# Idle products of the identity on TensorE between the two recurrences of a recommender kernel

## The chip, the cores and the metric

The kernel runs on one core of one Trainium2 chip. The metric is device time in microseconds (us) of the whole launch, the median of three runs. Below, PE is TensorE, DVE is VectorE, ACT is ScalarE, POOL is GpSimd and SP is SyncE. PEld is TensorE's weight load, and the clock is the share of TensorE's full speed that was granted.

## The reference

1024 users have a history of 100 items of 128 numbers each, in float32. A GRU runs over the history, an attention net scores its states against a query item, and a second recurrence (AUGRU) runs over the states with an attention weight a step. A small net ends it.

```python
_, gru_seq = jax.lax.scan(gru_step, h0, jnp.swapaxes(item_historical_embedding, 0, 1))
keys = jnp.swapaxes(gru_seq, 0, 1)
...
attn = jax.nn.softmax(score, axis=1)[..., 0]
pooled = jnp.einsum('bt,btd->bd', attn, keys)
att_seq = pooled.T[:T]

def augru_step(h, inp):
    x_t, a_t = inp
    ti = jnp.concatenate([h, x_t], axis=-1)
    r = jax.nn.sigmoid(ti @ aug_Wr.T + aug_br)
    u = jax.nn.sigmoid(ti @ aug_Wu.T + aug_bu)
    h_hat = jnp.tanh(jnp.concatenate([h * r, x_t], axis=-1) @ aug_Wh.T + aug_bh)
    u = a_t[:, None] * u
    h_new = (1.0 - u) * h + u * h_hat
    return (h_new, h_new)
_, aug_seq = jax.lax.scan(augru_step, h0, (jnp.swapaxes(keys, 0, 1), att_seq))
```

The weights a_t of the second recurrence are the columns of pooled, so step 0 of it needs pooled in full, which is known only when the first recurrence and the attention over all of its states are done. A user's result is the state at the end of his own history.

## The kernel before

The work has two phases, each a recurrence over 100 steps on two halves of 512 users. In the first, `gru_phase`, the GRU, the attention net and an online softmax run side by side; the states go to DRAM as keys_d. Its end (lines 888 to 956) empties the pipeline: the last attention scores, the last sums into pooled on POOL (half 0) and DVE (half 1), eight products of user features (`features`, line 630, PE's last work of the phase, in the two PSUM banks `banks["f"]`), and the store of pooled to DRAM as pooled_d.

The second, `augru_phase`, treats the users sorted by length, so that later steps are narrower. Between the phases stands a branch on a count of users, taken by every engine. Then, in the program's order:

- `load_key` (1047) for steps 0 to 3: PE transposes gathered states (L1055), ACT copies them to SBUF (L1056). `first_step` (986): gates of step 0 from the input alone, four products of 128x512 on PE (L996), sigmoid and tanh on ACT (L998).
- ACT issues three of the stores of pooled_d, SP the other five (L956). `gather_weights` (1002): POOL gathers rows of pooled_d in sorted order, four indirect DMAs a half (L144), as `att_r`. Then POOL gathers the states of later steps (L174), sixteen for half 1 with nothing between them, and from then on some each half step, each behind a copy (L173) that waits for DVE's `rest`, which sets their pace.
- `open_gates` (1068): the input's part of the three gates of step 1 (L1073). `close_gate` (1075) later adds the state's part (L1077).
- `first_state` (1019) for half 0: `weight_row` (1008) makes the row of weights of step 0 for 512 users by four row products with the identity (L1011), each of which waits for one gather; DVE multiplies it with the two gates (L1022, L1023), which gives the state after step 0. `first_weights` (1025): the same for step 1, copied by ACT (L1028).
- `half_step` (1088) for step 1 and half 0: products pr and pu on that state, sigmoids on ACT (L1097, L1098), DVE's r (L1103). `store_weights` (1030): PE transposes att_r (L1033), DVE copies it (L1035), SP stores it and loads the weights of later steps from there. Then `first_state` for half 1, with row products into the bank `spare`. In half 1's half step, `open_state` (1080) makes ph and its tanh (L1085), and pr and pu of half 1 follow, which read the state of L1023.

Each engine works in its program's order: on PE a product that waits holds all products behind it. In float32 a product is two records of the profile, a transpose one. The order is written by hand; waits are put in for it.

Of the kernel before, what the change touches and what calls it, by code (L numbers as in the profile page):

```python
# [19 lines left out]
P = 128  # L20
# [58 lines left out]
def kernel(ctx: ExitStack, tc: tile.TileContext, a: dict, out: bass.AP):  # L79
# [26 lines left out]
    nc = tc.nc  # L106
# [21 lines left out]
    ident = const.tile([P, P], F32, name="ident")  # L128
# [53 lines left out]
    def all_of(steps):  # L182
        for _ in steps:
            pass

    def gru_phase(pools):
        wih = const.tile([P, 3, P], F32, name="wih")
# [468 lines left out]
        def blocked(t):  # L656
            return t.rearrange("p (k r) -> p k r", r=R)
# [4 lines left out]
        banks = {}  # L662
# [164 lines left out]
        for s in range(T):  # L827
            last = s == T - 1
            n, due = divmod(s - again, 4)
            n, i = divmod(n, NH)  # L830
# [55 lines left out]
            if more_history and due == 2:  # L886
                halves[i].history(n)
        all_of(rest)

        b = [ps.tile([P, HB], F32, tag="g", name="last") for _ in range(6)]  # L890
# [23 lines left out]
        n = ENDS[-3] - ENDS[-4] + 1  # L914
# [30 lines left out]
        halves[0].pool(T, nc.gpsimd)  # L945
        halves[1].pool(T, nc.vector)
        all_of(more_early)


        for half in reversed(halves):  # L950
            t = blocked(s_bs[NH * (soft["j"] % 2) + half.i])
# [6 lines left out]
    def augru_phase(pools, widths, alive):  # L958
# [46 lines left out]
                gather(r[:, g, :], pooled_d, g, i)  # L1005
            return r

        def weight_row(t, i, p):

            for g in range(GH):  # L1010
                nc.tensor.matmul(  # L1011
                    p[:, ts(g, P)],
                    lhsT=sorted_rows[i][:, g, t : t + 1].to_broadcast([P, P]),
                    rhs=ident,
                    start=True,
                    stop=True,
                )

        def first_state(i, p):
            weight_row(0, i, p)  # L1020
            u, h = gates[i]
            nc.vector.tensor_mul(p, p, u)  # L1022
            nc.vector.tensor_mul(h3[i], p, h)  # L1023

        def first_weights(i, p):
            weight_row(1, i, p)
            at = att[1, i] = wp.tile([P, HB], F32, name="at", bufs=6)
            nc.scalar.copy(at, p)  # L1028
# [59 lines left out]
        def half_step(t, i):  # L1088
# [17 lines left out]
            if t == 1 and i == 0:  # L1106
                store_weights(0, pa.tile([P, HB], F32, tag="a", name="pw"))
                first_state(1, spare)
            elif t == 1:
                first_weights(1, spare)  # L1110
# [118 lines left out]
        for to, t in later["att", 0][: G - 1]:  # L1229
            nc.scalar.dma_start(out=to, in_=t)  # L1230
        sorted_rows = [gather_weights(i) for i in range(NH)]
        all_of(load_rows(1, 1, widths[FIRST[1]], kp))
        for i in range(NH):
            load_key(2, i, (FREE_BANK, None)[i])
        open_gates(1, 1, EARLY_BANKS)
        open_gates(1, 0, LATE_BANKS)
        for i in range(NH):
            load_key(3, i)
        spare = bank("spare", EARLY_BANKS[-1])
        first_state(0, pa.tile([P, HB], F32, tag="a", name="first"))  # L1240
        first_weights(0, spare)
        ahead, due = gathers(2), spread(2)
# [30 lines left out]
    with ExitStack() as pools, tc.manual_schedule():  # L1273
        gru_phase(pools)
# [79 lines left out]
```

## Time and profile before

| | us |
|---|---|
| median of three runs | 2048.63 |
| the three runs | 2044.19, 2048.63, 2048.96 |
| the profiled execution | 2046.78 |
| its span, first to last instruction | 2045.0 |
| PE busy | 1994.6 (98%) |
| DVE busy | 1682.1 (82%) |
| POOL busy | 1260.7 (62%) |
| ACT busy | 944.1 (46%) |
| mean granted clock of PE | 0.993 |
| last record of the first phase on PE ends | 1404.14 |
| first record of the steady second recurrence | 1460.53 |

The span runs from the first to the last instruction of the profiled execution, and all places are us from its start. A row of a group names line, engine, operation, what is written and read, shape and number of instructions. A time in brackets is idle time of the engine before the instruction, with what ended it.

### The profile page before, as it was taken

The numbers are of one execution on the slowest core, as the hardware profiler recorded it, in microseconds if no ns is written. First come the engines' busy times: TensorE is split into PE (matmuls) and PEld (weight loads), VectorE is DVE, ScalarE is ACT, GpSimd is POOL, SyncE is SP. The second block draws the span as 40 slices with busy tenths as digits, with TensorE's granted clock in tenths as the row PEclk, the third lists the DMA queues.
The fourth block names the chain that finished last, engine by engine and source line by source line (L and its number), as shares of the span: only waits on it lengthen the run. The fifth ranks groups of instructions, "written<-read, shape, count | busy, mean of one in ns | idle before, by whom it ended". The sixth has DMA issues, their size and how long they took to land.

```text
span 2045.0 us, 41241 instructions
## 1 busy us (share of the span) xinstructions
PE 1994.6 (98%) x15452; PEld 1176.7 (58%) x15452; DVE 1682.1 (82%) x3066; ACT 944.1 (46%) x1708; POOL 1260.7 (62%) x1291
## 2 busy tenths in 40 slices
PE   8999999999999999999999999997699999999997
PEld 3655555555555555555555555544344556679997
DVE  6888989888879887878888888996477777878886
ACT  4444444544544454544454444443244444445554
POOL 0233939579796959595969687997543344443431
PEclk9999999999999999999999999999899999999999
DMA  4553333332234334333433232333332333333322
GB/s 118 101 115 97 98 105 113 98 108 86 89 104 114 118 105 119 113 113 97 141 111 97 91 101 69 96 105 108 122 102 91 91 106 103 95 94 86 95 70 36
DMA packets 241645, 205.66 MB, mean 101 GB/s; under 512 B 59271, under 2 KB 204395, under 8 KB 241435
## 3 DMA queue, kind: packets, MB, share of 16 engines
q1 hardware_dynamic: 227498, 170.43, 29.4%
q0 software_dynamic: 12352, 32.31, 5.6%
q8 instruction: 123, 2.02, 0.4%
q14 instruction: 88, 0.71, 0.1%
q10 hardware_dynamic: 1584, 0.20, 0.1%
HBM read 146.82 MB, written 54.40 MB: 98 GB/s over the span
## 4 chain that ended last, share of the span: by engine, by line
PE 92%; DVE 3%; DMA 2%; issue 1%; ACT 1%; another core or an unknown queue 1%; POOL 0%; SPq 0%; DVEq 0%; ACTq 0%; POOLq 0%
PE ps L509 48%; PE pm L673 16%; PE ph L1077 5%; PE pr L1077 5%; PE pu L1077 4%; PE pu L1073 4%; PE ph L1073 4%; PE pr L1073 4%; DMA rows<-keys_d,idx_k 1%; DVE ps L539 0%; DVE u L529 0%; DVE ps L546 0%; DVE d L545 0%; DVE d L544 0%
## 5 line engine op out<-in xcount | busy, mean ns | idle before, releaser
L509 PE MATMUL ps<-x,wih 128*32 128x512 f32 x4800 | 657.2, 594 | 4.4 <-DMA x<-in_hist_x 4.4
L509 PE MATMUL ps<-hn,whh 128*32 128x512 f32 x4752 | 650.1, 592 | 0.6 <-ACT hn L555 0.6
L509 PEld LDWEIGHTS ps<-x,wih 128*32 128x32 f32 x4800 | 281.7, 110 | 241.7 <-issue 220.4
L509 PEld LDWEIGHTS ps<-hn,whh 128*32 128x32 f32 x4752 | 279.6, 110 | 234.2 <-issue 212.0
L494 POOL TENSOR_TENSOR xm<-x,m 128x512 f32<-128x512 f32 x200 | 234.9, 1174 | 146.0 <-DMA m<-mask_d 145.7
L521 ACT ACTIVATE r<-ps,brz 128x512 f32<-128x512 f32 x200 | 137.7, 688 | 394.9 <-PE ps L509 394.7
L495 POOL TENSOR_TENSOR hist<-hist,xm 128x512 f32<-128x512 f32 x200 | 258.7, 1294 | 15.7
L174 POOL DMA_INDIRECT rows<-keys_d,idx_k x220 | 213.2, 969 | 86.2 <-POOL rows L173 48.5
L610 POOL TENSOR_TENSOR pooled<-pooled,kw 128x512 f32<-128x512 f32 x191 | 245.9, 1287 | 15.0
L609 POOL TENSOR_TENSOR kw<-kt,e 128x512 f32<-128x512 f32 x191 | 206.0, 1078 | 70.6 <-DVE e L782 70.6
L673 PE MATMUL pm<-hn,wk 128*32 128x512 f32 x1200 | 237.7, 592 | 5.0 <-ACT hn L555 2.5
L673 PE MATMUL pm<-kq,wkq 128*32 128x512 f32 x1200 | 237.5, 592 | 0.0
L540 ACT ACTIVATE ps<-ps,bih 128x512 f32<-128x512 f32 x200 | 132.4, 662 | 223.9 <-DVE ps L539 223.9
L1085 ACT ACTIVATE c<-ph,bh 128x96 f32<-128x96 f32 (+41 forms) x198 | 96.5, 488 | 295.9 <-PE ph L1077 240.5
L529 DVE SCALAR_TENSOR_TENSOR u<-ps,bhh,r 128x512 f32<-128x512 f32 x198 | 147.5, 745 | 73.1 <-PE ps L509 69.0
L673 PE MATMUL pm<-mv,w 128*32 128x512 f32 (+1 forms) x808 | 197.6, 592 | 0.5 <-ACT mv L712 0.4
L173 POOL COPY rows<-rest 128x1 f32<-128x1 f32 x188 | 35.3, 188 | 217.5 <-DVE rest L1114 213.5
L544 DVE TENSOR_TENSOR d<-hn,ps 128x512 f32<-128x512 f32 x198 | 136.1, 687 | 35.6 <-ACT ps L540 35.2
L1101 DVE TENSOR_TENSOR pu<-pu,c 128x96 f32<-128x96 f32 (+41 forms) x197 | 88.3, 448 | 87.9 <-ACT c L1085 79.8
L545 DVE TENSOR_TENSOR d<-ps,d 128x512 f32<-128x512 f32 x200 | 138.4, 692 | 25.6 <-ACT ps L541 10.9
L555 ACT COPY hn<-ps 128x512 f32<-128x512 f32 x200 | 116.6, 583 | 92.3 <-DVE kq L548 92.3
L539 DVE TENSOR_TENSOR ps<-ps,u 128x512 f32<-128x512 f32 x200 | 140.0, 700 | 21.5 <-PE ps L509 0.5
(181 smaller groups left out, 3235.3 us busy)
## 6 DMA issues: line engine op xcount, KB each, us to landing
x<-in_hist_x SPq DMA_DIRECT2D x212, 256.0 KB
keys_d<-kt SPq DMA_DIRECT2D x48, 1024.0 KB
m<-mask_d SPq DMA_DIRECT2D x200, 128.0 KB
rows<-keys_d,idx_k POOLq DMA_INDIRECT x220
s_b<-mv SPq DMA_DIRECT2D x200, 8.0 KB
keys_d<-kt SPq DMA_DIRECT2D x32, 64.0 KB
at<-att_d SPq DMA_DIRECT2D x34, 48.0 KB
mask_i<-in_mask SPq DMA_DIRECT2D x8, 200.0 KB
```

The costliest lines, as they stand in the source:

```text
L174: nc.gpsimd.indirect_dma_start(out=r[:, at, :], out_offset=None, in_=keys_d[q], in_offset=bass.IndirectOffsetOnAxis(ap=idx_k[:, k, i : i + ...
L494: nc.gpsimd.tensor_mul(d, x, m)
L495: nc.gpsimd.tensor_add(acc, acc, d)
L509: nc.tensor.matmul(p[ts(q, R), :], lhsT=w[:, g, ts(q, R)], rhs=v, start=(j == 0), stop=(j == len(parts) - 1),)
L529: nc.vector.scalar_tensor_tensor(out=u, in0=ph, scalar=bhh[:, 2:3], in1=r, op0=ALU.add, op1=ALU.mult,)
L539: nc.vector.tensor_add(pi, pi, u)
L545: nc.vector.tensor_mul(d, pz, d)
L609: eng.tensor_mul(d, k, w)
L610: eng.tensor_add(acc, acc, d)
L673: nc.tensor.matmul(p[i][s, :], lhsT=w[:, s], rhs=v, start=start, stop=stop)
L1073: nc.tensor.matmul(p, lhsT=m[:, 1, :], rhs=k, start=True, stop=False)
L1077: nc.tensor.matmul(p, lhsT=m[:, 0, :], rhs=v, start=False, stop=True)
```

## The change

A helper issues products of the identity with itself into a PSUM tile. Nine of them follow PE's last product of the first phase, in the bank of an earlier one that has been copied out. Four precede each of the four row products of half 0 at step 0, in the quarter of the tile that the row product then overwrites. For half 1, and for the rows of step 1, none are added. Nothing reads what they write.

```diff
+    def busy(p, n):
+
+        for _ in range(n):
+            nc.tensor.matmul(p[:, :P], lhsT=ident, rhs=ident, start=True, stop=True)
...
         halves[1].pool(T, nc.vector)
         all_of(more_early)
 
+        busy(banks["f"][0], 9)
...
-        def weight_row(t, i, p):
+        def weight_row(t, i, p, idle=0):
 
             for g in range(GH):
+                busy(p[:, ts(g, P)], idle)
                 nc.tensor.matmul(
                     p[:, ts(g, P)],
                     lhsT=sorted_rows[i][:, g, t : t + 1].to_broadcast([P, P]),
...
         def first_state(i, p):
-            weight_row(0, i, p)
+            weight_row(0, i, p, 0 if i else 4)
```

## The prediction

> **What bounds the kernel now.** I read the page first, then the busy time by stage, then the chain of waits and each engine's order of time between 1404 and 1464 us. The page's 40 slices show TensorE (PE) full everywhere but at slices 28 and 29:
>
> ```profile
> PE   8999999999999999999999999997699999999997
> PEclk9999999999999999999999999999899999999999
> ```
>
> The second line, PE's granted clock, dips in the same place. By stage:
>
> ```profile
> 10.00:1378.00 1368.00, 1364.77 (x12708) 740.72 (x12699) 1175.97 (x1795) 646.68 (x1041) 964.28 (x819) 1.00 0.36 104
> 1404.00:1460.00 56.00, 32.43 (x103) 17.61 (x101) 18.32 (x37) 12.86 (x22) 40.39 (x43) 0.79 0.45 126
> 1460.00:2037.00 577.00, 569.87 (x2498) 403.04 (x2498) 464.93 (x1186) 271.12 (x622) 230.19 (x387) 1.00 0.34 91
> ```
>
> The first two columns are stage and length, the next PE's busy time, the seventh PEclk. Both recurrences are PE's (99.8% and 98.8% of their stages), at full clock. The 56 us between are not: 32 us of PE work. A microsecond won there reaches the end whole, since all later work is one PE chain. The clock in steps of 2 us:
>
> ```profile
> 1406.00:1408.00 2.00, 0.00 (x0) 0.00 (x0) 1.60 (x7) 1.51 (x5) 1.92 (x3) 0.97 1.12 354
> 1408.00:1410.00 2.00, 1.99 (x3) 0.96 (x4) 1.97 (x4) 1.25 (x1) 1.92 (x2) 0.50 0.97 294
> 1426.00:1428.00 2.00, 0.97 (x4) 0.59 (x4) 0.00 (x0) 0.00 (x0) 1.45 (x2) 1.00 0.19 51
> 1428.00:1430.00 2.00, 1.22 (x5) 1.22 (x6) 0.32 (x1) 0.00 (x0) 1.39 (x2) 0.59 0.19 47
> ```
>
> Each idle stretch (1405.0 to 1408.0; the gaps of 1424 to 1428) is followed by a half clock: 1407.87 to 1411.29, 1428.35 to 1435.18, and again 1442.01 to 1455.66. PE in order of time (start, length, idle time before it in brackets):
>
> ```profile
> 1425.30 0.46 PE L1011 MATMUL first<-ident,att_r 128*128 128x128 f32 x2 [1.28 <-DMA att_r<-pooled_d,idx]
> 1427.00 0.98 PE L1011 MATMUL first<-ident,att_r 128*128 128x128 f32 x4 [1.25 <-DMA att_r<-pooled_d,idx]
> 1428.78 0.79 PE L1011 MATMUL first<-ident,att_r 128*128 128x128 f32 x2 [0.80 <-DMA att_r<-pooled_d,idx]
> 1429.37 1.91 PE L1011 MATMUL spare<-ident,att_r 128*128 128x128 f32 x8
> ...
> 1435.39 1.06 PE L1011 MATMUL spare<-ident,att_r 128*128 128x128 f32 x8
> 1436.28 1.02 PE L1077 MATMUL ph<-r,wh 128*128 128x510 f32 x2
> 1450.17 2.07 PE L1077 MATMUL pr<-h,wr 128*128 128x510 f32 x2 [12.87 <-DVE spare L1022]
> ```
>
> A row product is two records. The reader should see that the three gaps the change fills are 3.3 us, and that a 12.87 us gap, four times as large, comes later. The chain of waits has it too:
>
> ```profile
> 1437.34 11.32 another core or an unknown queue
> 1448.69 0.71 DVE spare L1022
> ...
> 1454.28 4.19 another core or an unknown queue
> ```
>
> L1022 waits only for PE, for the four row products of half 1, whose records end by 1436.45. The trace's semaphore events tell more. PE's semaphore steps at 1434.94 (pu, on time), then 1436.63, 1437.37, 1440.91, 1445.14, 1448.67, 1453.57 and 1458.47. Matched in order, and by what DVE and ACT do next, these are pw, row products 0 to 3, ph, and pr of half 1. Their records end at 1435.55, 1435.78, 1436.00, 1436.22, 1436.45, 1437.30 and 1452.24, so PE's signals come 1 to 16 us late, one per 3.5 to 4.9 us. At 1459.27 all is caught up. POOL issues a gather every 1.26 us from 1422.48 to 1454.24, 26 on end; the delay starts some 12 us into that run and ends some 3 us behind it. Shorter runs late in the kernel (1822 to 1834, 1935 to 1946) also end with PE signals held, by up to 0.85 us. The trace names no cause.
>
> [...] these f32 records step by 111 and 213 ns, and I use those. [...]
>
> **The change part by part.** The instruction order of both programs shows 25 added products on the path taken and nothing else; the wait for ACT moves from the first row product to the first idle one. Form and price are those of a row product: 8 records in 0.89 us from 1435.39, so 0.22 us each at full clock; 8 in 1.71 us from 1429.37, so 0.43 us at half.
>
> Nine behind the first phase: 1403.98 + 9 x 0.22 = 1405.96. PE's branch work behind them (1401.87 to 1403.05 now) then waits for ACT's copy at 1402.83 + 0.33 and ends near 1404.4, under the idle products. The transposes of L1055 move from 1403.98 to 1405.96; the first four end at 1406.5, the rest at 1407.0. Their reader, ACT's L1056, starts at 1406.88 anyway, held by its own branch, and its second copy at 1407.4. Cost nothing; without ACT's branch as cover, 2.0 us. PE is then idle 1 us instead of 3, so the clock should hold: the four L996 products cost 3.4 us instead of 5.3. But ACT's k copies wait behind its DMA issues until 1417.94, and those wait for pooled. Worth nothing.
>
> Sixteen before half 0's row products: their tile is free at 1424.64. Four cost 0.88, row product 0 starts at 1425.5 (now 1425.30), row product 1 at 1427.0 (its gather), row product 2 at 1428.1, row product 3 at 1429.2 instead of 1428.78, but at full clock: it ends at 1429.6 as now (1429.58). Cost nothing at full clock, 16 x 0.43 - 3.3 of gaps = 3.6 us at half.
>
> Then, with the clock held to 1435: DVE delivers h at 1431.11 as now; pr's signal comes at 1432.1 instead of 1433.24, r at 1433.6 instead of 1434.65, pw at 1433.4, half 1's row products at 1434.0 (the last gather lands at 1433.49) instead of 1436.45. That is the step that matters: 1434.0 is before the delay sets in (1434.94 was on time). DVE's L1022 and L1023 end at 1435.7, and half 1's pr starts at 1435.8 instead of 1450.17.
>
> What is late next? The signals behind it, if the run of gathers, which the change leaves where it is, holds PE's signals whatever PE does. pr of half 1 would take the place of 1437.37, pu 1440.91, first_weights 1445.14, pw 1448.67, ph 1453.57, and pr of step 2 1458.47. Before, that last one came at 1463.8. Gain 5.3 us. The other bound: no delay at all. Then pu of step 2 (L1073, 1460.53) opens at 1439.3, a gain of 21.2. A bound below nothing is rival 4. I take 5.3, because the later runs of gathers show held signals with PE warm and busy.
>
> The sum is made against the profiled execution (2046.78, span 2045.0); the median is 1.85 above it. Differences go to the median: 2048.63 - 5.3 = 2043.3.
>
> **The rivals.**
> 1. Forecast, half a step won: 2043.3, its own range 2038 to 2047. For: the delay follows the run of gathers. Against: the later ones are shorter.
> 2. The delay goes, because it needs a cold or idle PE: 2048.63 - 21.2 = 2027.4. For: it begins at the clock's return at 1435.18 and lasts over an idle, cold PE; elsewhere PE is busy and the delays are under 1 us. Against: other returns of the clock (1411.29) show none.
> 3. The change does not do what it says: the clock falls anyway, or PE's time won is eaten by the same delay. Then half 1's row signals fall into it as now: 2047 to 2049, say 2048.
> 4. Slower: [...] PE is at half clock when the idle products start. Four cost 1.7 us before each row product, row product 3 ends 3.6 us later, at 1433.2, and pr and pu of half 0, on time now, fall into the delay as well. Two more signals wait some 4.2 us there, of which about 3 are left when it ends: 2048.63 + 3.6 + 3 = 2055. It decides if row product 3 ends after some 1431. [...] Against: the trace had the clock full until 1428.35.
>
> **How the numbers follow.** Chances: rival 1 0.36, rival 2 0.22, rival 3 0.22, rival 4 0.20. About 0.3% (6 us) is what a measurement can tell from no change. Half of 1 wins more than that: faster 0.18 + 0.22 = 0.40; same 0.18 + 0.22 = 0.40; slower 0.20. The range goes from rival 2, 2026, to most of rival 4, 2054; some 0.05 lies below, 0.12 above. Faster cases hold most of the chance.
>
> **What would show it.** Right: no half clock at 1407.87 and 1428.35; row product 3 ending near 1429.6; DVE's second L1022 near 1434.3 instead of 1448.69; the wait before ACT's L1097 of half 1 still of unknown origin (case 1) or gone (case 2). Wrong: L1055's ACT copies later than 1406.9, row product 3 later than 1431, or L1022 still near 1448.

## The result, and the profile after

| | before | after |
|---|---|---|
| median, us | 2048.2 (22 runs) | 2051.68 (22 runs) |
| lowest to highest | 2044.19 to 2050.77 | 2047.86 to 2053.26 |
| ratio, 95% interval | | 1.0017 [1.0011, 1.0023] |
| profiled execution | 2046.78 | 2053.26 |
| its span | 2045.0 | 2051.5 |
| last record of the first phase on PE starts | 1403.81 | 1405.89 |
| steady second recurrence opens (pu from the input, step 2) | 1460.53 | 1467.33 |

The change costs 3.5 us: slower by less than my 0.3% bound, and outside my likeliest case. In the kernel after, the lines named in the prediction are 7 higher (L1022 is L1029, L1028 is L1035, L1055 is L1062, L1077 is L1084, L1097 is L1104, L1103 is L1110); the idle products are L189.

The two profiled executions differ by 6.5 us in span. Of these, 2.08 lie ahead of the change: some 1.2 at a half clock of 3.4 us, 27 us into the kernel (26.8 to 30.2), where the trace before has none, and the rest in two small steps later in the first phase. Another 4.7 lie between the last record of the first phase and the steady second recurrence (56.7 and 61.4 us). The rest of the span is 0.3 shorter. So the 4.7 us are to be explained.

The 40 slices of the kernel after, PE's busy share and its clock, show the dip in the same place as before, with PE a tenth busier in one slice and the clock a tenth lower:

```profile
PE   8999999999999999999999999998699999999997
PEclk9999999999999999999999999999799999999999
```

The stages of 2 us (behind the stage, the second figure is PE's busy time and the seventh its clock) show that the idle products did their work. There is no half clock where the kernel before had 0.50 and 0.59, and PE is busy throughout 1428 to 1430:

```profile
1408.00:1410.00 2.00, 1.10 (x11) 0.86 (x9) 1.52 (x7) 1.48 (x4) 1.92 (x3) 1.00 1.12 353
1426.00:1428.00 2.00, 1.34 (x12) 1.20 (x11) 0.00 (x0) 0.57 (x1) 1.69 (x2) 1.00 0.23 66
1428.00:1430.00 2.00, 2.00 (x20) 2.00 (x19) 0.00 (x0) 0.00 (x0) 1.39 (x3) 1.00 0.12 33
```

PE in order of time, with the idle time before an instruction in brackets (the nine idle products are 18 records):

```profile
1406.06 2.17 PE L189 MATMUL last<-ident 128*128 128x128 f32 x18
1408.07 1.04 PE L1062 MATMUL pk<-ident,rows 128*128 128x128 f32 x8
...
1430.25 1.06 PE L189 MATMUL first<-ident 128*128 128x128 f32 x8
1431.14 0.48 PE L1018 MATMUL first<-ident,att_r 128*128 128x128 f32 x2
1431.46 1.06 PE L1018 MATMUL spare<-ident,att_r 128*128 128x128 f32 x8
1442.03 2.07 PE L1084 MATMUL pr<-h,wr 128*128 128x510 f32 x2 [9.51 <-issue]
1443.89 1.91 PE L1084 MATMUL pu<-h,wu 128*128 128x510 f32 x2
1445.59 1.06 PE L1040 MATMUL pw<-ident,att_r 128*128 128x128 f32 x4
1455.97 2.07 PE L1018 MATMUL spare<-ident,att_r 128*128 128x128 f32 x8 [9.32 <-ACT at L1035]
1460.16 2.07 PE L1084 MATMUL ph<-r,wh 128*128 128x510 f32 x2 [2.11 <-DVE r L1110]
1462.09 1.96 PE L1084 MATMUL pr<-h,wr 128*128 128x510 f32 x2
```

Row product 3 of half 0 (1431.14) ends at 1431.62, and the rows of first_weights follow right behind it. Then, where the kernel before ran pr at 1431.16, PE stands for 9.51 us. DVE's order of time tells whom pr waits for:

```profile
1440.55 0.70 DVE L1029 TENSOR_TENSOR first<-first,first_u 128x512 f32<-128x512 f32 x1 [22.16 <-remote]
...
1460.62 0.69 DVE L1029 TENSOR_TENSOR spare<-spare,first_u 128x512 f32<-128x512 f32 x1
```

The first of them in the kernel before:

```profile
1429.68 0.70 DVE L1022 TENSOR_TENSOR first<-first,first_u 128x512 f32<-128x512 f32 x1 [13.37 <-PE first L1011]
```

ACT's order of time in the kernel after:

```profile
1455.34 0.59 ACT L1035 COPY at<-spare 128x512 f32<-128x512 f32 x1 [28.59 <-remote]
```

What the first L1029 still lacks is row product 3, whose record has been over for 8.9 us; L1035 lacks first_weights, over since 1432.5. "Remote" says that no instruction of the trace ended shortly before the semaphore step that released them. The times of PE's semaphore steps, matched in order and by what DVE and ACT do next, tell more. After one at 1426.15 the next come at 1439.03 (of the last idle product, which steps the semaphore too), 1440.46 (row product 3) and 1455.19 (first_weights). Then come seven between 1458.70 and 1458.97, most of them some 43 ns apart: pr, pu and pw of half 0 and the four row products of half 1. The chain of waits puts it into one piece:

```profile
1426.52 28.67 another core or an unknown queue
```

So PE's signals are held (they reach their readers long after the record has ended) here as in the kernel before, but five more stand in the hold: those of the last idle product, of row product 3 and of first_weights, and behind them those of pr and pu of half 0, whose records end at 1444.10 and 1445.80. The hold ends as before, 4 to 5 us after POOL issues its last gather of the run (1453.66, released from 1458.70; before 1454.24 and 1458.47).

### The profile page after: what moved, and what is told of

Read it like the earlier page. It is cut to its first block, busy times and chain, and to the rows that moved or that the text cites. A ratio compares the mean times of both kernels' runs of the same rounds, so it can differ in the third digit from the quotient of the medians.

```text
span 2051.5 us, 41340 instructions
## 1 busy us (share of the span) xinstructions
PE 2000.3 (98%) x15502; PEld 1180.5 (58%) x15502; DVE 1681.0 (82%) x3066; ACT 943.7 (46%) x1708; POOL 1261.5 (61%) x1291
## 4 chain that ended last, share of the span: by engine, by line
PE 90%; DVE 5%; issue 2%; another core or an unknown queue 1%; ACT 1%; DMA 0%; ACTq 0%; SPq 0%; POOL 0%; DVEq 0%; POOLq 0%
PE ps L514 47%; PE pm L678 16%; PE ph L1084 5%; PE pr L1084 4%; PE pu L1080 4%; PE pu L1084 4%; PE pr L1080 4%; PE ph L1080 4%; DVE ps L544 0%; DVE u L534 0%; DVE ps L551 0%; DVE d L550 0%; ACT ps L545 0%; DVE d L549 0%
## 5 line engine op out<-in xcount | busy, mean ns | idle before, releaser
L514 PE MATMUL ps<-x,wih 128*32 128x512 f32 x4800 | 649.9, 595 | 4.1 <-DMA x<-in_hist_x 4.1
L514 PE MATMUL ps<-hn,whh 128*32 128x512 f32 x4752 | 642.0, 592 | 0.0
```

The source lines that it names most:

```text
L514: nc.tensor.matmul(p[ts(q, R), :], lhsT=w[:, g, ts(q, R)], rhs=v, start=(j == 0), stop=(j == len(parts) - 1),)
```

## The experiments

Runs made together share a chip, and the kernel before ran beside each. I call the five chips A to E in order of time; each was used once, so a chip cannot be told from its hour. All the idle products write what nothing reads, so no kernel here leaves anything out. One measure serves for all, from the profiles: the turn, from the start of the last record of the first phase on PE to the start of pu from the input for step 2. It was 56.7 us before and 61.4 after. "Lag" is DVE's first gate of the turn less the end of row product 3's record; where nothing is held it is 0.11 us.

**The two parts alone, and the gathers paced.** The nine and the sixteen are each left in alone. For the paced kernels, POOL's gathers of later states for half 1 are no longer issued in one go behind the attention weights, but handed out among the half steps:

```diff
-        all_of(load_rows(1, 1, widths[FIRST[1]], kp))
+        second = load_rows(1, 1, widths[FIRST[1]], kp)
...
-        ahead, due = gathers(2), spread(2)
+        def joined():
+            yield from second
+            yield from gathers(2)
+
+        ahead, due = joined(), [4, 4, 3, 3, 2] + [3] * 10 + [2]
```

e1_nine: after, with `weight_row(0, i, p)` in first_state. Expected:

> Only the nine idle products behind the first phase; none between the row products. Theory H (PE's signals are held while POOL issues its long run of gathers, and the change puts more of the critical signals into that hold): the nine lie under ACT's branch, so no change, 2048 us, ratio within 0.001 of 1; the second L1022 is as late as before, some 45 us behind the first phase's last product. Rival D (idle products cost their own time on PE's path): 2.0 us for the nine, 2050 us.

e2_sixteen: after, without `busy(banks["f"][0], 9)`. Expected:

> Only the sixteen idle products between half 0's row products. Theory H: all of the loss, 2051.5 us, with the signal of half 0's row product 3 held for some 9 us as in the changed kernel. Rival D: 16 x 0.22 less the 3.3 us of gaps, 0.3 us, so 2048.5 us, and the signal of row product 3 at its record's end.

e3_paced: before, paced. Expected:

> The kernel before, but the sixteen gathers of half 1's first states are not issued in one run: they join the paced ones, spread over five half steps of steps 1 to 3. Theory H: PE's signals come at their records' ends, the second L1022 some 34 us behind the first phase's last product instead of 45, the waits of unknown origin gone: 15 to 21 us faster, about 2030 us. Rival C (the signals are late because PE is cold and idle there, whatever POOL does): the waits stay, 2048 us.

e4_paced_idle: after, paced. Expected:

> The changed kernel with the same paced gathers as e3_paced. Theory H: as e3_paced within 1.5 us, since with the hold gone the idle products are covered, and perhaps 1 to 2 us faster than it from the clock held full: 2029 us. Rival C: the idle products keep the clock up to 1436, so the waits shrink here and not in e3_paced. Rival D: 2 to 3 us slower than e3_paced.

Measured on chip A, where before took 2018.32 us:

| | us | ratio | turn | lag |
|---|---|---|---|---|
| e1_nine | 2019.3 | 1.000 [0.9992, 1.0008] | 37.8 | 0.11 |
| e2_sixteen | 2017.74 | 0.9997 [0.9989, 1.0006] | 36.4 | 0.11 |
| e3_paced | 2018.81 | 1.0003 [0.9995, 1.0012] | 37.9 | 0.11 |
| e4_paced_idle | 2018.75 | 1.0001 [0.9992, 1.0009] | 36.4 | 0.11 |

That was not foreseen: the same kernel before is 30 us faster here than in the first measurement, and in none of the four traces is a signal held in the turn. What the expectations said of held signals could not be judged on this chip. What could: only the kernels with the sixteen have a shorter turn (36.4, against 37.8 with the nine alone, and 37.9 in the kernel before on chip B, below).

**Both kernels again, and a price.** Is it the chip? r_before and r_after are the two kernels unchanged, r_paced is e3_paced again, and e5_twelve has `0 if i else 12` in place of `0 if i else 4`.

> The kernel before again, with a profile, on the chip of this call. The four runs before this took some 30 us less than the blind comparison, the kernel before with them, and their traces show no held PE signals. Theory S (the held signals belong to the chip or the hour, not to the kernel): either about 2018 us with no wait of unknown origin in the turn between the phases, or about 2048 us with such waits of 10 us and more; nothing between. Rival K (they belong to the kernel before and after alone, and each of the four edits happened to remove them): waits of unknown origin and 2048 us here in any case.

> The changed kernel again beside r_before. Theory S: without held signals 1.4 us shorter in the turn (last product of the first phase to pr of half 1: 32.2 us instead of 33.6), ratio 0.9993; with them 1.0017 again, and the signal of half 0's row product 3 held. Rival K: 2051 us in any case.

> The kernel before with half 1's sixteen gathers paced, as in e3_paced. If r_before shows held signals here: theory H (POOL's run of gathers holds them) says 15 us or more less than r_before, rival C (a cold PE) no less. If it shows none: within 0.1% of r_before, as in e3_paced.

> The changed kernel with twelve instead of four idle products before each of half 0's row products. 12 x 0.22 = 2.68 us and 0.22 us for the row product, against a gather every 1.26 us. Theory P (row product 3 stands behind all idle products of its kind on PE, whatever has landed): it starts at the tile's release + 4 x 2.68 + 3 x 0.22, 7.2 us later than with four, and as PE's work of 5 us there is all on the path, the kernel is 7 us slower than r_after. Rival: PE lets a row product that is ready past, or the cover is longer than I read: under 3 us.

On chip B, before took 2018.95 us:

| | us | ratio | turn | lag |
|---|---|---|---|---|
| r_before | 2019.81 | 1.0000 [0.9992, 1.0009] | 37.9 | 0.11 |
| r_after | 2016.89 | 0.9990 [0.9983, 0.9997] | 36.4 | 0.11 |
| r_paced | 2019.08 | 1.0002 [0.9994, 1.001] | 37.8 | 0.11 |
| e5_twelve | 2024.83 | 1.0026 [1.0016, 1.0035] | 43.6 | 0.11 |

The kernel after is faster here, by 2 us, of which the turn has 1.4; on chip A the sixteen alone were not clear of no change (0.9997). DVE's order of time in r_after has both gates where the prediction wanted them, with nothing remote. Its first phase ends 1.1 us earlier than in the trace that the prediction used, so the second gate stands at 1434.4 on that scale, where 1434.3 was forecast:

```profile
1428.40 0.70 DVE L1029 TENSOR_TENSOR first<-first,first_u 128x512 f32<-128x512 f32 x1 [13.21 <-PE first L1018]
...
1433.23 0.70 DVE L1029 TENSOR_TENSOR spare<-spare,first_u 128x512 f32<-128x512 f32 x1 [0.20 <-PE spare L1018]
```

In e5_twelve, thirty-two more idle products than in r_after lengthen the turn by 7.2 us and the time by 7.9. At 0.22 us each they should cost 7.0, so the price holds. No row product passed the idle products ahead of it, or the cost would not be whole. And 10.6 us of idle products (48 of them) are not enough to make a signal late on chip B.

**Pacing where signals are held.** The paced kernel and the kernel after once more:

> The kernel before with half 1's sixteen gathers paced, on whichever chip this call gets. If the kernel before takes some 2048 us here, the held signals are back: theory H (POOL's run of gathers holds PE's signals) says 15 us or more less than the kernel before and no wait of unknown origin between the phases; rival C (a cold, idle PE holds them) says about the same as before, with the waits. If the kernel before takes some 2018 us here, within 0.1% of it, and nothing is told apart.

> The changed kernel on the same chip. Where the kernel before takes some 2048 us: 1.0017 of it, with half 0's signals held. Where it takes some 2018 us: 0.9993 of it or a little less, with PE's clock full through the turn.

This time the chip (C) held signals; before took 2044.22 us. s1_paced: 2026.15, ratio 0.9911 [0.9895, 0.9928], turn 37.4, lag 0.11. s2_after: 2049.03, 1.0021 [1.0015, 1.0028], turn 60.7, lag 6.71. POOL in s1_paced (start, length) stops behind the eighth attention gather, where the kernel before goes on without a pause until 1454.24:

```profile
1430.56 0.95 POOL L144 DMA_INDIRECT att_r<-pooled_d,idx  x1 [0.30 <-issue]
1431.82 0.95 POOL L144 DMA_INDIRECT att_r<-pooled_d,idx  x1 [0.30 <-issue]
1438.73 0.18 POOL L173 COPY rows<-rest 128x1 f32<-128x1 f32 x1 [5.96 <-DVE rest L1114]
```

and PE's half 1, which waited 12.87 us before, waits for DVE's own work only:

```profile
1437.28 1.12 PE L1077 MATMUL pr<-h,wr 128*128 128x510 f32 x2 [0.66 <-DVE h L1023]
```

Pacing takes 18 us off the time (four runs against 23), though it took nothing off where no signal is held. The turn is 37.4, much as on the chips without a hold; that of the kernel before has no trace from this chip, and was 56.7 in its first one. So the hold is bound to the run of gathers (to their issue on POOL or to the transfers that they start, which no run tells apart), and s1_paced is faster than both kernels. It is still 7 us slower than r_paced on chip B, and in the traces some 6 of these lie behind the turn.

**Which part brings the hold forward.** The parts alone once more, one idle product per row instead of four (`0 if i else 1`), and after with pacing:

> The nine idle products alone, without the sixteen. Where before reads about 2044 us or more and holds PE's signals: if it is the sixteen products that bring the hold forward (theory S), row product 3 of half 0 is signalled on time, DVE's first gate of the turn runs near 1433, the hold begins behind it as before, and the ratio is 0.999 to 1.001. If any idle product that holds the clock does it (rival N), DVE's first gate comes after 1437 and the ratio is 1.001 to 1.003. Where before reads about 2019, no hold, ratio 1.000, as measured once.

> The sixteen idle products alone, without the nine. Where PE's signals are held: theory S expects the loss whole, ratio 1.0015 to 1.003, with DVE's first gate of the turn waiting until after 1436 for a row product that ended by 1432. Rival N expects the ratio of before, 0.999 to 1.001. Where they are not held, ratio 0.9997, as measured once.

> The kernel after with one idle product instead of four behind each row product of half 0 (four in all). Where PE's signals are held: if the number of products ahead of row product 3's signal counts, its signal comes on time and the ratio is 0.999 to 1.001; if one is enough, ratio 1.0015 to 1.003. Where they are not held, within 0.001 of before.

> The kernel after with the gathers paced among the steps: both remedies together. Theory H (the hold is bound to the unpaced run of gathers): where PE's signals are held, about 2025 us beside 2044, ratio 0.990 to 0.992, and with the clock kept full up to 2 us better than the paced kernel alone. Rival: the idle products bring a hold with them whatever the gathers do, ratio 0.995 or more. Where they are not held, ratio 0.999 to 1.0005.

Chip D held signals too; before took 2044.11 us:

| | us | ratio | turn | lag |
|---|---|---|---|---|
| t1_nine | 2043.72 | 1.0002 [0.9994, 1.0011] | 54.3 | 0.11 |
| t2_sixteen | 2049.43 | 1.0028 [1.0016, 1.0041] | 61.7 | 5.31 |
| t3_one | 2044.47 | 1.0005 [0.9997, 1.0014] | 56.7 | 0.11 |
| t4_paced_idle | 2031.03 | 0.9941 [0.9925, 0.9958] | 43.1 | 4.69 |

The sixteen alone cost as much as the whole change; the nine, and one product a row, cost nothing. DVE in t1_nine, then in t2_sixteen (whose lines are one lower):

```profile
1427.81 0.70 DVE L1029 TENSOR_TENSOR first<-first,first_u 128x512 f32<-128x512 f32 x1 [13.30 <-PE first L1018]
...
1445.82 0.70 DVE L1029 TENSOR_TENSOR spare<-spare,first_u 128x512 f32<-128x512 f32 x1 [11.21 <-remote]
```

```profile
1434.34 0.70 DVE L1028 TENSOR_TENSOR first<-first,first_u 128x512 f32<-128x512 f32 x1 [18.46 <-remote]
...
1456.64 0.69 DVE L1028 TENSOR_TENSOR spare<-spare,first_u 128x512 f32<-128x512 f32 x1
```

With the nine, only the second gate waits for something unknown, as before; with the sixteen it is the first gate, and all that follows it.

t3_one shows one thing more. Its row products of half 1 end at 1435.07, 1.4 us earlier than before (0.3 of it from ahead of the turn), and the gate that reads them is as late as before:

```profile
1437.22 0.69 DVE L1042 COPY att_t<-pw 128x512 f32<-128x512 f32 x1 [2.92 <-PE ph L1084]
1448.44 0.70 DVE L1029 TENSOR_TENSOR spare<-spare,first_u 128x512 f32<-128x512 f32 x1 [10.53 <-remote]
```

The first late signal is that of pw, whose record ends at 1434.17 and whose reader is the copy at 1437.22 (its bracket names ph, the last PE record that had ended by then). In the kernel before and in t1_nine the first late signal is pw's too.

t4_paced_idle was a miss for my theory. I had expected 0.990 to 0.992, because pacing should leave nothing to hold signals; yet DVE's first gate is held even by the eight attention gathers alone:

```profile
1432.83 0.70 DVE L1029 TENSOR_TENSOR first<-first,first_u 128x512 f32<-128x512 f32 x1 [17.87 <-remote]
```

It comes 1.7 us after the last of those gathers ends (1431.13), and PE's signals are on time soon after. The theory that fits these runs is that a run of gathers holds PE's signals while it lasts and a little longer (4 to 5 us behind the last issue above, 1.7 behind the end of the last gather here), and that how soon within it depends on what PE does.

**Count or pauses?** With four idle products a row PE no longer pauses for a gather ahead of the row products (0 us in the kernel after); with none or one it does (3.3 us in the kernel before, 1.6 in t1_nine, 0.5 in t3_one). Three kernels were to tell the pauses from the count: products 32 columns wide instead of 128 (`rhs=ident[:, :32]`), two a row, and none ahead of row product 3 (`idle if g < GH - 1 else 0`). u4_paced_nine is paced, with the nine and without the sixteen.

> The kernel after with its sixteen idle products 32 columns wide instead of 128: the same count, about a quarter of the work. Where before reads 2044 us or more and PE's signals are held: if it is PE running without a pause through the attention gathers that brings the hold ahead of half 0's row product 3 (theory D), PE waits for the gathers again, DVE's first gate of the turn runs within 1 us of row product 3's record, and the ratio is 0.999 to 1.001. If it is the count of products ahead of the signal (rival C), that gate comes 3 us or more behind the record and the ratio is 1.0015 to 1.003. Where no signal is held, ratio 0.999 to 1.001 for both.

> The kernel after with two idle products instead of four ahead of each row product of half 0. Where PE's signals are held: theory D expects PE to wait a little for gathers still, 0.2 to 1 us in all, the signal on time and the ratio 0.999 to 1.001; rival C expects something between one product (1.0005) and four (1.002 to 1.003). Where none is held, ratio 0.999 to 1.001.

> The kernel after without the four idle products ahead of row product 3 of half 0 (twelve stay). Where PE's signals are held: theory D in its narrow form (the pause just ahead of the signal counts) expects the signal on time and the ratio 0.999 to 1.001; if the three dense rows ahead are enough, or the count, the signal is held and the ratio is 1.0015 to 1.003. Where none is held, ratio 0.999 to 1.001.

> The nine idle products with the gathers paced and without the sixteen. Where PE's signals are held: as the sixteen are what brought a hold back into the paced kernel, this one has none in the turn and is like the paced kernel alone, ratio 0.990 to 0.9925, with the clock full from the first phase's end to the row products. If pacing fails with any idle product, ratio 0.994 or more. Where none is held, ratio 0.999 to 1.001.

Chip E held nothing; before took 2018.94 us:

| | us | ratio | turn | lag |
|---|---|---|---|---|
| u1_narrow | 2020.49 | 1.0008 [0.9999, 1.0017] | 40.5 | 0.11 |
| u2_two | 2017.34 | 0.9993 [0.9984, 1.0002] | 36.4 | 0.11 |
| u3_not_last | 2017.67 | 0.9992 [0.9983, 1.0001] | 36.6 | 0.11 |
| u4_paced_nine | 2019.62 | 1.0005 [0.9998, 1.0012] | 38.0 | 0.11 |

So the question stays open. What the four runs add: two products a row give as short a turn as four do (36.4), and narrow ones a longer one (40.5). PE in u1_narrow shows that they were not the quarter of the work that I had counted on:

```profile
1424.22 1.08 PE L188 MATMUL first<-ident 128*128 128x32 f32 x8 [0.67 <-ACT k L1067]
1425.13 0.47 PE L1022 MATMUL first<-ident,att_r 128*128 128x128 f32 x2
1425.44 0.98 PE L188 MATMUL first<-ident 128*128 128x32 f32 x8
1426.25 0.73 PE L1022 MATMUL first<-ident,att_r 128*128 128x128 f32 x2
1426.78 1.75 PE L188 MATMUL first<-ident 128*128 128x32 f32 x8
```

Eight records of 32 columns take 0.98 to 1.08 us, of 128 columns 1.06 to 1.16 (L189 above). But they did not keep the clock: it was half from 1426.3 to 1436.5, and the third eight took 1.75. So this kernel would not have told count from pauses as meant.

## Why the prediction was wrong, step by step

- **The nine behind the first phase: right.** L1062 moved by 2 us, ACT's copy L1063 did not (0.04 beside the first phase's own 2.08), and the clock stayed full (1.00) through 1408 to 1411. That it would, with PE idle for 1 us (1.03 measured), was my estimate; the length of a pause alone does not decide, for in the kernel before pauses of 1.28 and 1.25 us had a half clock behind them (1428.35), and in the kernel after one of 1.59 (ahead of 1420.69) had none. Worth nothing, as the ratio of both runs with the nine alone says (1.000 and 1.0002).
- **Sixteen before the row products, at full clock: right.** Row product 3 ended 2.04 later than before, in an execution that was 2.08 later ahead of it. Four idle products took 0.89 us, 0.22 each. That they would keep the clock full was my estimate, from a trace in which each half clock came behind pauses of PE or in one; the stages above bear it out (1.00 from 1426 to 1430, in place of 1.00 and then 0.59). How busy PE must be for it was not shown.
- **"1434.0 is before the delay sets in (1434.94 was on time)": the step that failed.** It took the hold's start for a fixed place, some 12 us into POOL's run of gathers, out of one trace. That place is not fixed. Even without the four idle products a row, the hold began earlier where PE's work came earlier. The first late signal was pw's each time; its record ended 13.1 us into the run in the kernel before, 12.1 in t1_nine and 11.9 in t3_one, and the gate behind half 1's row products stood 25 to 26 us into the run in all three. With the four, it begins far earlier still. Below, the end of row product 3's record is given as us from the first gather of the run, on the chips that held signals, with its lag:

| | idle per row | row product 3 ends | lag |
|---|---|---|---|
| before | 0 | 7.1 | 0.11 |
| s1_paced | 0 | 7.4 | 0.11 |
| t1_nine | 0 | 7.2 | 0.11 |
| t3_one | 1 | 7.2 | 0.11 |
| after | 4 | 6.9 | 8.9 |
| s2_after | 4 | 6.9 | 6.7 |
| t2_sixteen | 4 | 6.9 | 5.3 |
| t4_paced_idle | 4 | 6.7 | 4.7 |

  The place in the run is nearly the same; only the four idle products a row divide on time from late. The hold starts earlier because of the change itself, before 1431.3 in the kernel after. The work that I meant to bring ahead of the hold was not ahead of it.
- **"What is late next?": right as a question, short by five signals.** I moved six signals along the old list of release times. Those of the last idle product, of row product 3, of first_weights, and of pr and pu of half 0 came to stand ahead of them. (The idle product's own step is not the cause: t3_one has one too, and its row product 3 was on time.) DVE's first gate came 10.9 us later than before (1440.55 against 1429.68). Not all of that reaches the end, since the release 4 to 5 us after the run's last gather ends the wait in both: at the opening of the steady recurrence 6.8 us are left, 2.08 of them from ahead of the change.
- **Rival 2, no delay (2027.4): its mechanism was wrong.** The hold does not need a PE that is cold (at half clock) or idle. PE was at full clock (1.00) and busy without a pause, from 1426.80 to 1432.5, when it began in the kernel after. Without a hold the change is worth 1.4 us of turn and a ratio of 0.9990 in its one measurement, not 21 us, because nearly all of those 21 us (18.9 between the two traces of the kernel before) are lost to the hold and not to the clock.
- **Rival 3, the same time:** nearest in size (+0.17%), but not the case: the signals that were late were others.
- **Rival 4, slower (2055): its sign was right, and its result was near by luck, for its reason was wrong.** No half clock stood ahead of the row products (1.00 from 1424 to 1432). What it named behind that, that pr and pu of half 0 fall into the delay, is what happened, but by way of the held signal of row product 3. Its point of decision, row product 3 later than some 1431, was not the cause: in t2_sixteen it ended at 1429.03, as far behind the first phase as in the kernel before (25.7 and 25.8 us), and was held all the same.

Shown: where signals are held, the loss is that of the sixteen products, through held signals of row product 3 and of first_weights; where none are held, the change is worth at most a little (0.9990 and, for the sixteen alone, 0.9997); and pacing the gathers without the sixteen frees the turn of the hold and wins 18 us. Not shown: why four idle products a row bring the hold forward (the missing pauses, their number, or something else), what holds a signal at all, and whether it is the chip or the hour that decides. One rival stands untested: the recording of the trace itself. Each execution here was recorded, and all traces from the chips that held signals, s1_paced among them, lack records: they have 2163 to 2179 of PE's steps on one semaphore, against 2307 to 2310 on the other chips, and the steps of ACT and DVE lack a like share. In the kernel before, 126 of PE's 135 missing steps lie behind 1700 us, in the second recurrence with its gathers. So gathers, missing records and held signals go together, and it is open whether an execution that is not recorded has a hold at all.

## What to carry to other kernels

Before you fill an idle stretch, ask whether the engine behind it waits for the work or for the signal: a record that has long ended, ahead of a reader released by "remote" or by "an unknown queue", points to a signal that comes late, and doing the work sooner need not bring it sooner (in t3_one the row products of half 1 ended 1.4 us sooner, and their gate was as late). When the start of such a delay is read from one trace, take it for a property of that trace, and price the case in which the change moves it. Here the remedy with the larger effect lay on another engine, POOL's gathers handed out instead of issued in one run (0.9911 where signals were held, 1.0003 where none were).

## What was not expected of the hardware

- The kernel before took 2044 to 2048 us in three measurements and 2018 to 2019 in three others (chips A, B and E). Between r_before and the first profile of the kernel before, 18.9 us of the 27.0 of span lie in the turn (37.9 and 56.7), and the rest nearly all in the second recurrence behind it, which gathers too.
- PE's semaphore steps came up to 16 us late before (ph, record over at 1437.30, step at 1453.57) and up to 23 us in the kernel after (first_weights, 1432.52 and 1455.19).
- Products of the identity with 32 columns instead of 128 cost nearly the same time (0.98 to 1.08 us for eight records, against 1.06 to 1.16), and did not keep the clock full where those of 128 columns did (half clock from 1426.3, against none ahead of the gates in u2_two; mean clock 0.994 and 0.997). They filled PE as well: it was busy for 2.72 of the 3.41 us ahead of that half clock, while the kernel before kept the full clock behind 1421.53 to 1424.94 with 1.83 of 3.41. (3.41 us is the stretch because the half clocks in the traces before and after, but for the one at the end of each, are one, two, three or four times as long: 3.41, 6.83, 10.24 and 13.65.)
- Eight gathers, of 0.95 us with 0.30 between, were enough to hold a signal for 4.7 us with four idle products a row (t4_paced_idle), and held none without them (s1_paced).
